# A two-layer convolution kernel: the fill of layer 0 in a written order

## The chip, the cores and the metric

The kernel runs on one core of a Trainium2 chip. The engines are named as the profile names them: PE (TensorE, matrix products; PEld is its weight load), DVE (VectorE), ACT (ScalarE), POOL (GpSimd) and SP (SyncE, which here only issues DMAs; ACT issues some too). The metric is the device time of one execution in microseconds, and of several executions the median.

## What is computed

The input `x` is two images of 512 channels and 64 x 64 pixels, float32. Two layers follow each other, both with a group norm in front and a residual:

```
x = x + L0(_gn(x))       # _gn: 32 groups, mean and variance over channels of a group and all pixels
x = x + L1(_gn(x))

L0:  xproj  = x^T @ in_w + in_b                       # 512 -> 512 per pixel
     x1     = depthwise 3x3 conv of x, + dw_b         # per channel
     x1     = gelu(layernorm over channels(x1) * ln_g + ln_b)
     offset = x1 @ off_w + off_b                      # 16 groups x 9 points x 2
     mask   = softmax over 9 points of (x1 @ mask_w + mask_b)
     out    = bilinear samples of zero-padded xproj at 9 shifted points, weighted by mask
     out    = out @ out_w + out_b

L1:  q, k   = tanh(x Wq^T), tanh(x Wk^T);  attn = softmax(q diag(align_w) k^T) over 4096 pixels
     out    = relu(batchnorm((x + attn @ (x Wv^T)) Wfc^T + bfc))
```

## The kernel before

**Tiling.** Channels lie on 128 partitions in `KB` = 4 blocks. An image is cut into `NCH` = 8 chunks of `CH` = 512 pixels (`ROWS` = 8 image rows), so layer 0 has `NSEQ` = 16 chunks. All of it is float32. `window_path` (the function that the change touches) does layer 0 and then layer 1; a second path for unusual data, `general_path`, is not taken here.

**Stages of layer 0**, each a Python generator whose `yield`s cut it into steps:

- `image_stats(n)`: a `bn_stats` (L723) for each of 32 pieces of an image, `bn_aggr` for each channel block, and the small chain of `group_norm_steps` (L609 to L627: two tiny products with `gmat`, a root on ACT), which leaves scale and bias (L731, L732). Image 0 is loaded whole at the start into `img` (L661, L662: two tiles lie over `bt`, two in the `patch` slots) and its statistics read that. Image 1's pieces come one by one by ACT-issued DMAs (L721) into three places (`early` twice, and `xraw`).
- `project(i)`: chunk i with a row above and below is normalized on ACT into `xn` (L758; there is one `xn` for all chunks), then four products `pq` with `in_w` (L768), each copied by ACT to one of two `xj` tiles (L774) and stored to `xt_d` in DRAM (L776). Chunk 0 reads its pixels from `img`; all other chunks load them again into `raw` tiles (L747).
- `features(i)`: the depthwise convolution of `xn` into `a` (tag `conv`, one buffer): tap 1 on ACT (L793), eight more taps for each channel block on DVE (L798), a sum over blocks on POOL (L804, L806), the mean by a product with `ones` on PE (L811), subtraction (L816, DVE), squares (L819, ACT), sums (L822, L824, POOL), the variance on PE, its root (L828, ACT), reciprocal and scaling (L830, L831, DVE), Gelu (L835, ACT) into `feat` (one buffer).
- `weights(i)`: four products `po` with the offset and mask weights (L852), bias (L857, DVE), exponential (L864, ACT), tent functions and products (L869 to L900, DVE), a copy (L903, ACT) and transposes (L911, PE).
- `fetch(i, s)`: SP loads 8 patches from `xt_d` into a `patch` tile (L924).
- `sample(i)`: spreads the weights (`pb` L940, `bt` L945), gathers by products with the patches (`pa` L959, copies L970), applies `out_w` (`py` L979), adds the input (L984), takes layer 1's statistics (L985) and stores.
- `value_weights()`: layer 1's product of `Wv` and `Wfc`: `wv` and `wf` are loaded (L1106, L1107) into the two `dT` buffers, and four groups of products `pw` (L1111) are copied to `res` tiles (L1115) and stored.
- `output_bias()`: `in_b` through `out_w` (L1123), added to `out_b`.

The zero padding of the projected image is made by the 16 stores of `edge` (L701, L702) into the border of `xt_d`.

**Order.** Within `tc.manual_schedule()` every engine gets its instructions in the order in which the program is traced. There, `period` interleaves four chunks: sampling of chunk i (`m`), weights of i+1 (`w`), features of i+2 (`f`), projection of i+3 (`p`), the rest of the chunk before (`y`, `v`), and six calls of `more`, each a step of image 1's statistics. Outside of it a planner puts the traced instructions of each engine in an order of its own, after its own model of their times. The fill, which brings chunks 0 to 2 to where the first period begins, is planned in this way:

```
run(image_stats(0), project(0), value_weights(), features(0), project(1))
v = Chain(weights, 0)
v(23)
run(features(1), project(2), output_bias())
fetch(0, 0)
fetch(0, 1)
later, y, f = image_stats(1), Chain(sample, NSEQ), Chain(features, 2)
with tc.manual_schedule():
    f()
    for i in range(NSEQ):
        if i == NCH - 3:
            run(later)
```

`Chain(stage, i)(k)` runs the next k steps of a stage. At i = 5 the remaining steps of image 1's statistics run at once, because chunk 8, the first of image 1, is projected in that period.

Of the kernel before, what the change touches and what calls it, by code (L numbers as in the profile page):

```python
# [9 lines left out]
F32 = mybir.dt.float32  # L10
# [7 lines left out]
P = 128  # L18
NB = 2
C = 512  # L20
KB = C // P
H = W = 64
# [8 lines left out]
CH = 512  # L31
NCH = S // CH
ROWS = CH // W
# [537 lines left out]
def window_path(ctx: ExitStack, tc: tile.TileContext, t_in: dict, out: bass.AP, far: bass.AP, sums: bass.AP):  # L571
# [12 lines left out]
    def load(name, shape, src=None, pool=const, **kw):  # L584
        t = pool.tile(shape, F32, name=f"{name}_sb", **kw)
        nc.sync.dma_start(t, t_in[name] if src is None else src)
        return t
# [49 lines left out]
    with ExitStack() as l0:  # L637
# [39 lines left out]
        nc.gpsimd.tensor_copy(om_b, om_b0.rearrange("p (a g k) -> p a k g", a=3, k=NP))  # L677
        out_w = load_w("L0_conv_out_w", C, wp)
        out_b = load("L0_conv_out_b", [P, KB], None, wp)
        ones = wp.tile([P, P], F32, name="ones_c")  # L680
        nc.vector.memset(ones, 1.0 / C)

# [10 lines left out]
            id32[:, :NW].rearrange("p (y x) -> p y x", x=5),  # L693
        )

        edge = io.tile([P, C], F32, tag="res", name="edge", bufs=4)
        nc.sync.dma_start(edge, t_in["L0_conv_in_b"].partition_broadcast(P))
        nc.vector.tensor_scalar(edge, edge, -1.0, None, ALU.mult)
        for n in range(NB):
            for e in (0, 1, WIN - 2, WIN - 1):  # L700
                nc.sync.dma_start(xt_d[n][e], edge[:WIN, :])  # L701
                nc.sync.dma_start(xt_d[n][2 : H + 2, e, :], edge[:H, :])  # L702

        gn = {}

        def image_stats(n):

            mv = sm.tile([P, KB, 2], F32, name="gn_mv")
            room = [early[:, 0], early[:, 1], io.tile([P, CH], F32, name="xraw")] if n else []
            pieces, ahead = deque((kb, h) for kb in range(KB) for h in range(NCH)), deque()  # L710
            for kb in range(KB):
                st = sm.tile([P, NCH, 6], F32, name="gn_st")
                for h in range(NCH):
                    if n == 0:
                        t = img[kb][:, h * CH : (h + 1) * CH]
                    else:

                        while len(ahead) < 3 and pieces:
                            k2, h2 = pieces.popleft()
                            ahead.append(room[len(pieces) % 3])  # L720
                            nc.scalar.dma_start(ahead[-1], x_v[n, :, k2, h2 * CH : (h2 + 1) * CH])  # L721
                        t = ahead.popleft()
                    nc.vector.bn_stats(st[:, h, :], t)  # L723
                    yield
                nc.vector.bn_aggr(mv[:, kb, :], st.rearrange("p a b -> p (a b)"))
            yield
            result = []
            yield from group_norm_steps(mv, KB, sm, ps, result)
            sc, bi = result
            gn[n] = [sm.tile([P, KB], F32, name=f"gn_{k}{n}") for k in ("scale", "bias")]  # L730
            nc.vector.tensor_copy(gn[n][0], sc)  # L731
            nc.vector.tensor_copy(gn[n][1], bi)  # L732

        def project(i):

            n, ch = divmod(i, NCH)
            sc, bi = gn[n]
            lo, hi = max(ch * ROWS - 1, 0), min(ch * ROWS + ROWS + 1, H)
            r0 = lo - (ch * ROWS - 1)
            raws = deque()  # L740

            def read(kb):
                if i == 0:
                    raws.append(img[kb][:, lo * W : hi * W].rearrange("p (r c) -> p r c", c=W))
                else:
                    t = io.tile([P, ROWS + 2, W], F32, name="raw", bufs=3)
                    nc.sync.dma_start(t[:, : hi - lo, :].rearrange("p r c -> p (r c)"), x_v[n, :, kb, lo * W : hi * W])  # L747
                    raws.append(t[:, : hi - lo, :])

            for kb in range(3):  # L750
                read(kb)
            yield
            if ch == 0:
                nc.gpsimd.memset(xn[:, :, 0, :], 0.0)
            if ch == NCH - 1:
                nc.gpsimd.memset(xn[:, :, ROWS + 1, :], 0.0)
            for kb in range(KB):
                nc.scalar.activation(  # L758
                    xn[:, kb, r0 : r0 + hi - lo, :], raws.popleft(),
                    AF.Identity, bias=bi[:, kb : kb + 1], scale=sc[:, kb : kb + 1],  # L760
                )
                if kb + 3 < KB:
                    read(kb + 3)
                yield
            for t in range(ROWS // 2):
                pq = ps.tile([P, C], F32, tag="mm", name="pq")
                for kb in range(KB):
                    nc.tensor.matmul(  # L768
                        pq, xn[:, kb, 1 + 2 * t : 3 + 2 * t, :].rearrange("p r c -> p (r c)"), in_w[:, kb, :],
                        start=(kb == 0), stop=(kb == KB - 1),  # L770
                    )
                yield
                xj = io.tile([P, C], F32, name="xj", bufs=2)
                nc.scalar.copy(xj, pq)  # L774
                for r in range(2):
                    nc.sync.dma_start(xt_d[n][2 + ch * ROWS + 2 * t + r, 2 : W + 2, :], xj[r * W : (r + 1) * W, :])  # L776
                yield
# [2 lines left out]

        def features(i):

            a = cv.tile([P, KB, CH], F32, tag="conv", name="conv")
            def tap_of(kb, tap):
                dy, dx = tap // 3, tap % 3 - 1
                acc = a[:, kb, :].rearrange("p (r c) -> p r c", c=W)
# [4 lines left out]
            for kb in range(KB):  # L791
                dst, src, wt = tap_of(kb, 1)
                nc.scalar.activation(dst, src, AF.Identity, bias=dw_b[:, kb : kb + 1], scale=wt)  # L793
            yield
            for kb in range(KB):
                for tap in (0, 2, 3, 4, 5, 6, 7, 8):
                    dst, src, wt = tap_of(kb, tap)
                    nc.vector.scalar_tensor_tensor(dst, src, wt, dst, ALU.mult, ALU.add)  # L798
                    if tap < 8:
                        yield  # L800

                if kb == 1:
                    tot = sm.tile([P, CH], F32, tag="tot", name="tot")
                    nc.gpsimd.tensor_add(tot, a[:, 0, :], a[:, 1, :])  # L804
                elif kb > 1:
                    nc.gpsimd.tensor_add(tot, tot, a[:, kb, :])  # L806
                yield
# [181 lines left out]
        def run(*generators):  # L989
            for gen in generators:  # L990
                for _ in gen:
                    pass
# [109 lines left out]

        def value_weights():

            wv, wf = [cv.tile([P, KB, C], F32, tag="dT", name=name, bufs=2) for name in ("wv", "wf")]
            nc.sync.dma_start(wv, t_in["L1_conv_Wv"].rearrange("(kb p) m -> p kb m", p=P))  # L1106
            nc.sync.dma_start(wf, t_in["wfcT"].rearrange("(kb p) m -> p kb m", p=P))  # L1107
            for cb in range(KB):
                pw = ps.tile([P, C], F32, tag="mm", name="pw")
                for kb in range(KB):  # L1110
                    nc.tensor.matmul(  # L1111
                        pw, wv[:, kb, cb * P : (cb + 1) * P], wf[:, kb, :], start=(kb == 0), stop=(kb == KB - 1)
                    )
                t = io.tile([P, C], F32, tag="res", name="wc_part", bufs=4)
                nc.scalar.copy(t, pw)  # L1115
                nc.sync.dma_start(wc_d[:, cb, :], t)
                yield
# [9 lines left out]
            nc.vector.tensor_add(out_b, out_b, pb[:, :KB])  # L1127
            yield

        run(image_stats(0), project(0), value_weights(), features(0), project(1))  # L1130
        v = Chain(weights, 0)
        v(23)
        run(features(1), project(2), output_bias())
        fetch(0, 0)
        fetch(0, 1)
        later, y, f = image_stats(1), Chain(sample, NSEQ), Chain(features, 2)
        with tc.manual_schedule():
            f()
            for i in range(NSEQ):
                if i == NCH - 3:  # L1140
                    run(later)
                    for k, name in enumerate(("wkT", "wqT", "wkT")):
                        nc.sync.dma_start(wkq[:, :, k, :], t_in[name].rearrange("(kb p) m -> p kb m", p=P))
                    for h in range(2):
                        nc.sync.dma_start(al[h * DQ : (h + 1) * DQ, :], t_in["L1_conv_align_w"])
                w, m, g = Chain(weights, i + 1), Chain(sample, i), Chain(features, i + 3)
                if i + 2 >= NSEQ:
                    (next_to_last if i + 1 < NSEQ else last_period)(y, v, m, w)
                    y, v = m, w
                    continue  # L1150
                period(y, v, m, w, f, g, Chain(project, i + 3), lambda: next(later, None))
                y, v, f = m, w, g
            y.rest()

# [442 lines left out]
```

## Time and profile before

| | us |
|---|---|
| median of 3 runs | 3677.05 |
| lowest and highest | 3676.55, 3680.48 |
| the profiled execution | 3680.32 |
| its span, first to last instruction | 3678.2 |

| engine | busy us | share of the span |
|---|---|---|
| PE | 3412.8 | 93% |
| DVE | 2351.4 | 64% |
| ACT | 1306.7 | 36% |
| POOL | 292.7 | 8% |

The mean granted TensorE clock is 0.973. A timeline has start and duration in us, engine, line, operation, output and inputs, and in brackets the idle time of the engine before it with what ended it. "SPq" and "ACTq" are DMA issues on SP and ACT. A table of stretches has from left to right the stretch, its length, busy time (and count) of PE, PEld, DVE, ACT and POOL, the granted clock, the busy share of the DMA engines, and GB/s. A list of waits has who waited for whom, the sum in us, how often, and the longest. The float32 products count as two records each on PE.

### The profile page before, as it was taken

To read this page: it belongs to the slowest core of one execution; us is meant where nothing else is said; L and a number is where in the kernel's file an instruction comes from. 1 tells how busy PE (TensorE), PEld (TensorE's weight loads), DVE (VectorE), ACT (ScalarE), POOL (GpSimd) and SP (SyncE) were. 2 spreads that over 40 slices of the span, in tenths; PEclk is the share of its full clock that TensorE was granted. 3 is DMA by queue.
4 is the path that set the end of the run, shared out by engine and by line. 5 is a ranking of instruction groups with operands and counts; after the bars stand their busy time and mean duration, and the time that the engine had idled before them with its cause. 6 is when DMAs were issued, how large, how long until landed. Compare 5 with 4: busy or idle time off the path is not lost.

```text
span 3678.2 us, 38948 instructions
## 1 busy us (share of the span) xinstructions
PE 3412.8 (93%) x15155; PEld 2432.7 (66%) x15155; DVE 2351.4 (64%) x3549; ACT 1306.7 (36%) x1694; POOL 292.7 (8%) x190
## 2 busy tenths in 40 slices
PE   4689998999998999999999999999999999999990
PEld 1355555555555677777777777777777777777770
DVE  5699999999997575554554554477455455545544
ACT  2477786887886421111111111121111111111114
POOL 2112111212111020000000000021000000000000
PEclk9799999999999999999999999999999999999995
DMA  7233442442432445334333433434333343343349
GB/s 241 66 98 112 142 138 83 121 128 85 129 107 71 154 171 180 124 103 163 122 119 134 143 123 113 153 146 187 130 126 116 115 139 112 102 150 122 112 177 379
DMA packets 175044, 499.92 MB, mean 136 GB/s; under 512 B 21600, under 2 KB 55136, under 8 KB 165376
## 3 DMA queue, kind: packets, MB, share of 16 engines
q1 hardware_dynamic: 166464, 462.72, 37.2%
q10 hardware_dynamic: 8352, 34.61, 2.6%
q8 instruction: 121, 1.98, 0.2%
q14 instruction: 75, 0.61, 0.0%
q0 software_dynamic: 32, 0.00, 0.0%
HBM read 405.96 MB, written 91.29 MB: 135 GB/s over the span
## 4 chain that ended last, share of the span: by engine, by line
PE 78%; DVE 13%; DMA 4%; ACT 2%; issue 1%; POOL 1%; SPq 1%; ACTq 0%; DVEq 0%; POOLq 0%
PE acc L1423 42%; DVE conv L798 9%; PE pS L1268 7%; PE p L1466 6%; PE py L979 5%; PE pq L768 5%; PE pa L959 5%; PE pv L1308 3%; PE pk L1362 1%; PE p_mean L811 1%; DVE o L857 1%; DMA v<-wv 1%; DMA in_w<-in_L_conv_in_w 1%; DMA xraw<-in_x 0%; DMA r<-wc 0%
## 5 line engine op out<-in xcount | busy, mean ns | idle before, releaser
L1423 PE MATMUL acc<-e,v 128*128 128x256 f32 x3072 | 768.3, 386 | 0.0
L1272 ACT ACTIVATE e<-pS 128x1024 f32<-128x1024 f32 x256 | 262.1, 1024 | 1386.9 <-PE pS L1268 1318.4
L1423 PE MATMUL acc<-tt,v 128*128 128x256 f32 x3072 | 748.2, 380 | 0.9 <-DMA v<-wv 0.9
L1423 PEld LDWEIGHTS acc<-e,v 128*128 128x128 f32 x3072 | 566.8, 190 | 232.9 <-issue 165.3
L1423 PEld LDWEIGHTS acc<-tt,v 128*128 128x128 f32 x3072 | 582.7, 190 | 91.4 <-issue 10.6
L1275 DVE TENSOR_TENSOR t<-e 128x256 f32<-128x256 f32 x256 | 109.0, 426 | 762.3 <-ACT e L1272 762.3
L798 DVE SCALAR_TENSOR_TENSOR conv<-xn,L_conv_dw_w_sb,conv 128x504 f32<-128x504 f32 (+1 forms) x512 | 400.2, 796 | 42.8 <-ACT conv L793 30.8
L1285 DVE TENSOR_TENSOR tot<-tot,e 128x512 f32<-128x512 f32 x480 | 330.2, 688 | 8.3
L959 PEld LDWEIGHTS pa<-bt,patch 96*128 96x128 f32 x2048 | 252.6, 198 | 62.2 <-issue 34.8
L1268 PE MATMUL pS<-q,kq 64*128 64x512 f32 x1024 | 289.0, 641 | 0.0
L959 PE MATMUL pa<-bt,patch 96*128 96x128 f32 x2048 | 256.3, 282 | 12.2 <-ACT dT L970 5.8
L945 ACT COPY bt<-pb 96x1024 f32<-96x1024 f32 x124 | 234.6, 2007 | 61.2 <-PE pb L940 52.3
L768 PE MATMUL pq<-in_w,xn 128*128 128x512 f32 x512 | 236.4, 606 | 4.0 <-ACT xn L758 4.0
L979 PE MATMUL py<-dT,L_conv_out_w_sb 128*128 128x512 f32 x512 | 236.1, 606 | 0.0
L1466 PE MATMUL p<-t,v 128*128 128x256 f32 x1024 | 231.4, 382 | 1.1 <-DMA v<-wv 1.1
L1466 PEld LDWEIGHTS p<-t,v 128*128 128x128 f32 x1024 | 192.3, 190 | 47.6 <-issue 21.2
L970 ACT COPY dT<-pa 32x256 f32<-32x256 f32 x496 | 179.5, 362 | 69.1 <-PE pa L959 60.3
L852 PE MATMUL po<-om_w_pg,feat 128*128 128x432 f32 x512 | 203.3, 543 | 0.0
L979 PEld LDWEIGHTS py<-dT,L_conv_out_w_sb 128*128 128x128 f32 x512 | 98.2, 196 | 118.9 <-issue 115.0
L768 PEld LDWEIGHTS pq<-in_w,xn 128*128 128x128 f32 x512 | 94.4, 195 | 109.0 <-issue 93.1
L852 PEld LDWEIGHTS po<-om_w_pg,feat 128*128 128x128 f32 x512 | 93.8, 192 | 90.9 <-issue 89.9
L1268 PEld LDWEIGHTS pS<-q,kq 64*128 64x128 f32 x1024 | 77.1, 184 | 84.9 <-issue 84.9
(206 smaller groups left out, 3730.9 us busy)
## 6 DMA issues: line engine op xcount, KB each, us to landing
v<-wv SPq DMA_DIRECT2D x252, 768.0 KB
patch<-xt SPq DMA_DIRECT2D x256, 192.0 KB
v<-wv SPq DMA_DIRECT2D x256, 128.0 KB
wv<-v SPq DMA_DIRECT2D x32, 896.0 KB
xt<-xj SPq DMA_DIRECT2D x128, 128.0 KB
res<-in_x SPq DMA_DIRECT2D x64, 256.0 KB
wx<-res SPq DMA_DIRECT2D x64, 256.0 KB
xq<-wx SPq DMA_DIRECT2D x16, 1024.0 KB
```

The source lines that it names most:

```text
L768: nc.tensor.matmul(pq, xn[:, kb, 1 + 2 * t : 3 + 2 * t, :].rearrange("p r c -> p (r c)"), in_w[:, kb, :], start=(kb == 0), stop=(kb == KB ...
L798: nc.vector.scalar_tensor_tensor(dst, src, wt, dst, ALU.mult, ALU.add)
L852: nc.tensor.matmul(po[:, : 3 * GP], f[:, kb, t * P : (t + 1) * P], om_w[:, kb].rearrange("p a k g -> p (a k g)"), start=(kb == 0), stop=(k ...
L945: copy(bt[:SN].rearrange("s g q d -> s d (g q)")[:, d0 : d0 + 4, :], pb[:SN])
L959: nc.tensor.matmul(pa[:, p], xp[:SN, p, cb * P : (cb + 1) * P], bt[:SN, 4 * cb : 4 * cb + 4, PX * s + p, :], start=True, stop=True,)
L970: copy(dst, src)
L979: nc.tensor.matmul(py, out_w[:, kb, cb * P : (cb + 1) * P], dT[:, kb, :], start=(kb == 0), stop=(kb == KB - 1))
L1268: nc.tensor.matmul(pS[:, h, :], kq[r, 2 * (kp // 4) + h, c0 : c0 + P], qs[qb][r, :], start=True, stop=True)
L1272: nc.scalar.activation(e.rearrange("p a q -> p (a q)"), pS.rearrange("p h q -> p (h q)"), AF.Exp)
L1285: nc.vector.tensor_add(tots[qb], tots[qb], e2[:, h, :])
L1423: nc.tensor.matmul(acc[j][:, cb * HQ : (cb + 1) * HQ], v[:, j, cb * P : (cb + 1) * P], ops[j], start=(kp + cb == 0), stop=(kp + cb == NPAI ...
L1466: nc.tensor.matmul(p7[:, cb * HQ : (cb + 1) * HQ], v7[:, cb * P : (cb + 1) * P], t3, start=(k + cb == 0), stop=(k + cb == NPAIR + 2),)
```

## The change

The fill is written out by hand. Only the loads, small preparations and `image_stats(0)` stay with the planner. The parts:

- `wv` and the four quarters of `wf` are loaded at the start, ahead of `edge`: `wv` into a `dT` buffer, `wf` into the four `res` tiles. `value_weights` makes its four quarters one at a time, where it is called, and copies them to `xj` tiles instead of `res`.
- `edge` lies in a `raw` tile, and its 16 stores are a function `border`, called after chunk 0's projection.
- Chunks 0, 1 and 2 all read their pixels from `img`.
- The convolution of chunk 1 has a buffer of its own (a `dT` slot), and its sum over channels lies in a `raw` tile, so that it can be made while chunk 0's convolution is still normalized.
- `features(0)` and `features(1)` yield after each block of tap 1, so that the blocks of normalization and tap 1 alternate on ACT.
- `image_stats(1)` has one more step, which sends the first three loads; it and eight pieces are taken in the fill.

The diff without its unchanged lines and some renamings:

```diff
+        wv = cv.tile([P, KB, C], F32, tag="dT", name="wv", bufs=2)
+        nc.sync.dma_start(wv, t_in["L1_conv_Wv"].rearrange("(kb p) m -> p kb m", p=P))
+        wf = [io.tile([P, C], F32, tag="res", name="wf", bufs=4) for _ in range(KB)]
+        for kb in range(KB):
+            nc.sync.dma_start(wf[kb], t_in["wfcT"][kb * P : (kb + 1) * P, :])
...
-        edge = io.tile([P, C], F32, tag="res", name="edge", bufs=4)
+        edge = io.tile([P, ROWS + 2, W], F32, name="raw", bufs=3).rearrange("p r c -> p (r c)")[:, :C]
         nc.sync.dma_start(edge, t_in["L0_conv_in_b"].partition_broadcast(P))
         nc.vector.tensor_scalar(edge, edge, -1.0, None, ALU.mult)
-        for n in range(NB):
-            for e in (0, 1, WIN - 2, WIN - 1):
-                nc.sync.dma_start(xt_d[n][e], edge[:WIN, :])
-                nc.sync.dma_start(xt_d[n][2 : H + 2, e, :], edge[:H, :])
+        def border():
+            for n in range(NB):
+                for e in (0, 1, WIN - 2, WIN - 1):
+                    nc.sync.dma_start(xt_d[n][e], edge[:WIN, :])
+                    nc.sync.dma_start(xt_d[n][2 : H + 2, e, :], edge[:H, :])
...
+            def refill():
+                while len(ahead) < 3 and pieces:
+                    k2, h2 = pieces.popleft()
+                    ahead.append(room[len(pieces) % 3])
+                    nc.scalar.dma_start(ahead[-1], x_v[n, :, k2, h2 * CH : (h2 + 1) * CH])
+            if n:
+                refill()
+                yield
...
-                if i == 0:
+                if i < 3:
                     raws.append(img[kb][:, lo * W : hi * W].rearrange("p (r c) -> p r c", c=W))
...
-            a = cv.tile([P, KB, CH], F32, tag="conv", name="conv")
+            a = cv.tile([P, KB, CH], F32, tag="dT", name="conv", bufs=2) if i == 1 else cv.tile([P, KB, CH], F32, tag="conv", name="conv")
...
-            yield
+                if i < 2 or kb == KB - 1:
+                    yield
...
+                    if i == 1:
+                        tot = io.tile([P, ROWS + 2, W], F32, name="raw", bufs=3).rearrange("p r c -> p (r c)")[:, :CH]
+                    else:
+                        tot = sm.tile([P, CH], F32, tag="tot", name="tot")
...
-                t = io.tile([P, C], F32, tag="res", name="wc_part", bufs=4)
+                t = io.tile([P, C], F32, tag="xj", name="wc_part", bufs=2)
...
-        run(image_stats(0), project(0), value_weights(), features(0), project(1))
-        v = Chain(weights, 0)
-        v(23)
-        run(features(1), project(2), output_bias())
-        fetch(0, 0)
-        fetch(0, 1)
+        run(image_stats(0))
         later, y, f = image_stats(1), Chain(sample, NSEQ), Chain(features, 2)
+        def more():
+            next(later, None)
         with tc.manual_schedule():
+            p0, p1, p2 = [Chain(project, i) for i in range(3)]
+            f0, f1, v, products = Chain(features, 0), Chain(features, 1), Chain(weights, 0), value_weights()
+            p0()
+            for kb in range(KB):
+                p0()
+                f0()
+            for t in range(4):
+                p0(2)
+                f0(8)
+            border()
+            more()
...
```

The remaining calls are, in this order (one call to a word, the number of steps in brackets): p1(3), f1, product, p1, f1(2), product, p1, f1, f1(6), f0(2), p1(4), f1(12), f0, p1(2), f0, p1, f0(2), p1, f1(14), product, p2(5), f; four times v, more, more, v; fetch of both patch tiles of chunk 0; f1, v, f1, v, p2(2), v(2), p2(2), v, f1, v(3), p2(2), f1, p2, f1(2), p2, v(6), product, output bias, v. The step counts: `project` has 1 to 5 for reading and normalizing and then two for each of four products; `features(0)` and `features(1)` have 4 for tap 1, 32 for the taps on DVE, then mean, squares, root, scaling, and two for Gelu. The periods follow as before, with `more` in them.

More of the change, by code (lines that the diff above doesn't have):

```diff
@@ L716, in image_stats @@
                     else:
[L718 to L721, printed above, removed]
+                        refill()
                         t = ahead.popleft()
@@ L802, in features @@
                 if kb == 1:
-                    tot = sm.tile([P, CH], F32, tag="tot", name="tot")
+                    if i == 1:
+                        tot = io.tile([P, ROWS + 2, W], F32, name="raw", bufs=3).rearrange("p r c -> p (r c)")[:, :CH]
+                    else:
+                        tot = sm.tile([P, CH], F32, tag="tot", name="tot")
                     nc.gpsimd.tensor_add(tot, a[:, 0, :], a[:, 1, :])
@@ L1103, in value_weights @@
         def value_weights():
-            wv, wf = [cv.tile([P, KB, C], F32, tag="dT", name=name, bufs=2) for name in ("wv", "wf")]
-            nc.sync.dma_start(wv, t_in["L1_conv_Wv"].rearrange("(kb p) m -> p kb m", p=P))
-            nc.sync.dma_start(wf, t_in["wfcT"].rearrange("(kb p) m -> p kb m", p=P))
             for cb in range(KB):
@@ L1111, in value_weights @@
                     nc.tensor.matmul(
-                        pw, wv[:, kb, cb * P : (cb + 1) * P], wf[:, kb, :], start=(kb == 0), stop=(kb == KB - 1)
+                        pw, wv[:, kb, cb * P : (cb + 1) * P], wf[kb], start=(kb == 0), stop=(kb == KB - 1)
                     )
-                t = io.tile([P, C], F32, tag="res", name="wc_part", bufs=4)
+                t = io.tile([P, C], F32, tag="xj", name="wc_part", bufs=2)
                 nc.scalar.copy(t, pw)
@@ L1128, in output_bias @@
             yield
-        run(image_stats(0), project(0), value_weights(), features(0), project(1))
-        v = Chain(weights, 0)
-        v(23)
-        run(features(1), project(2), output_bias())
-        fetch(0, 0)
-        fetch(0, 1)
+        run(image_stats(0))
         later, y, f = image_stats(1), Chain(sample, NSEQ), Chain(features, 2)
+        def more():
+            next(later, None)
         with tc.manual_schedule():
-            f()
+            p0, p1, p2 = [Chain(project, i) for i in range(3)]
[9 more added lines that the diff above has]
+            more()
+            p1(3)
+            f1()
+            next(products)
+            p1()
+            f1(2)
+            next(products)
+            p1()
+            f1()
+            f1(6)
+            f0(2)
+            p1(4)
+            f1(12)
+            f0()
+            p1(2)
+            f0()
+            p1()
+            f0(2)
+            p1()
+            f1(14)
+            next(products)
+            p2(5)
+            f()
+            for t in range(4):
+                v()
+                more()
+                more()
+                v()
+            fetch(0, 0)
+            fetch(0, 1)
+            f1()
+            v()
+            f1()
+            v()
+            p2(2)
+            v(2)
+            p2(2)
+            v()
+            f1()
+            v(3)
+            p2(2)
+            f1()
+            p2()
+            f1(2)
+            p2()
+            v(6)
+            next(products)
+            run(output_bias())
+            v()
             for i in range(NSEQ):
@@ L1150, in window_path @@
                     continue
-                period(y, v, m, w, f, g, Chain(project, i + 3), lambda: next(later, None))
+                period(y, v, m, w, f, g, Chain(project, i + 3), more)
                 y, v, f = m, w, g
```

## The prediction

> **What bounds the kernel now.** I read the slices of the span first, then busy time by stretches, then VectorE's (DVE's) waits and its instructions in order of time in the fill, and last the queues that its releasers stand in.
>
> ```profile
> PE   4689998999998999999999999999999999999990
> DVE  5699999999997575554554554477455455545544
> ...
> 0.00:92.00 92.00, 40.23 (x76) 17.48 (x77) 49.72 (x89) 18.46 (x27) 25.38 (x20) 0.91 0.70 241
> 92.00:184.00 92.00, 56.13 (x169) 28.59 (x167) 64.36 (x73) 41.86 (x47) 13.32 (x9) 0.74 0.24 66
> 251.00:322.00 71.00, 65.99 (x308) 38.98 (x308) 66.78 (x79) 54.01 (x73) 13.04 (x9) 0.98 0.41 130
> 1240.00:1900.00 660.00, 652.34 (x2798) 495.43 (x2798) 365.87 (x672) 123.09 (x156) 29.48 (x12) 1.00 0.41 144
> ```
>
> A slice is 92 us. From slice 3 DVE stands at 9 (a period of 71 us has 66.8 us of it: 94%), from about 1240 us TensorE (PE) at 99%. Only the first two slices are loose: DVE has 49.7 and 64.4 us of 92, and no other engine is full. So the fill is a matter of order and waits; whatever it sheds reaches the end, because a full engine follows all the way. Where DVE stands still:
>
> ```profile
> DVE conv L816 <- PE p_mean L811: 18.1, 1, 18.1
> DVE rstd L830 <- ACT rstd L828: 13.2, 2, 8.1
> DVE conv L798 <- ACT conv L793: 11.4, 2, 7.5
> DVE L_conv_out_b_sb L1127 <- PE p_bias L1123: 8.7, 1, 8.7
> DVE gn_st L723 <- DMA early<-in_x: 5.9, 1, 5.9
> ...
> 36.11 0.43 DVE L698 TENSOR_SCALAR edge<-edge 128x512 f32<-128x512 f32 x1 [1.38 <-DMA edge<-in_L_conv_in_b]
> 40.60 21.14 DVE L798 SCALAR_TENSOR_TENSOR conv<-xn,L_conv_dw_w_sb,conv 128x504 f32<-128x504 f32 x32 [3.91 <-ACT conv L793]
> 79.84 2.29 DVE L816 TENSOR_TENSOR conv<-conv,p_mean 128x2048 f32<-128x2048 f32 x1 [18.09 <-PE p_mean L811]
> 179.06 0.69 DVE L723 BATCH_NORM_STATS2 gn_st<-early 128x6 f32<-128x512 f32 x1 [5.87 <-DMA early<-in_x]
> 246.21 3.09 DVE L798 SCALAR_TENSOR_TENSOR conv<-xn,L_conv_dw_w_sb,conv 128x504 f32<-128x504 f32 x4 [3.02 <-ACT conv L793]
> ```
>
> The 18.09 us before L816 come from elsewhere:
>
> ```profile
> 51.33 11.54 POOL L804 TENSOR_TENSOR tot<-conv 128x512 f32<-128x512 f32 x1 [16.62 <-DVE conv L798]
> 56.24 0.54 SPq L1107 DMA_DIRECT2D wf<-in_wfcT  x1
> 62.35 16.59 PE L1111 MATMUL pw<-wf,wv 128*128 128x512 f32 x32 [7.70 <-issue]
> ```
>
> SP sends 16 border stores from 36.6 to 52.4, then pixel stores, and only at 56.2 wf. All 32 records of the weight product wait for it on PE, and p_mean, whose sum is ready at 65.6, starts at 78.8. One more loose place lies past the fill:
>
> ```profile
> 534.14 1.28 ACT L622 ACT_TABLE_LOAD   x1
> 535.76 0.18 DVE L625 RECIPROCAL gn_sc<-gn_var 128x4 f32<-128x4 f32 x1 [4.62 <-ACT gn_var L622]
> ```
>
> There the rest of image 1's statistics runs in one piece: the first taps of successive convolutions lie 71.2 us apart (317.02, 388.22), this one 76.8 behind its forerunner (459.45 by the chain of waits, to 536.25).
>
> **What the Trainium skill says.** "SBUF — State Buffer", section "Who interferes with whom": a DVE instruction with two SBUF inputs and a GpSimd (POOL) instruction that reads SBUF exclude each other for a whole instruction. The trace agrees: the add at 51.33 took 11.54 us beside DVE's unbroken taps against 1.26 us alone; later, taps held up by an add take 1.66 instead of 0.74 us. "VectorE: DVE Perf Modes", section "The DRAIN you can't avoid": a semaphore after each operation costs a chain nothing. Here it differs: at 40.60 taps of two channel blocks alternate (the 504 and 512 shapes come in pairs) and each takes 0.66 us; at 179.67 and 246.21 taps of one block follow each other, at 0.78. "DMA: Bandwidth & Descriptors", section "Queues, rings and completion order": SP's and ACT's queues take turns on the same DMA engines. The trace: at 324.6 an ACT piece of 256 KB took 6.16 us beside SP's patches, at 176.1 one took 2.98.
>
> **The change, part by part**, as DVE's queue, which is what the fill waits for.
>
> *Loads.* wv and four wf, 2.1 MB, now stand before edge on SP. From 27 to 36 us the queue moved about 0.33 MB per us, so edge lands 6.3 us later, at 42.4, and L698 ends at 42.9. All later DVE work queues behind it. ACT's normalization needs 1.6 us from 36.7 to the first tap at 38.3, so 4.6 us are lost if L698 stands last in the unwritten part, and 6.8 if it stays before the copies L731 and L732 as now. I take 42.9. The product's operands are then there before it is called.
>
> *First convolution.* Written block by block: 32 taps at 0.78, 24.8, plus two POOL adds at 0.9: 42.9 to 69.5. That is 3.7 slower than the alternating order, but without POOL's starvation. PE's 13.8 us of pq and ACT's four copies lie beside it; the border's 16 stores come behind the pixel stores, about 57 to 73.
>
> *Second convolution between.* It has its own buffer (the dT slot of om_b) and its own sum, so while the first waits for means DVE does its taps. Six taps 4.7 + 0.9: 75.1 (first means: sum 70.8, matmul 72.9, hidden). L816 2.2: 77.3. Twelve taps 9.4 and four POOL adds 3.6: 90.3; beside them the squares, POOL, the variance and ACT's root, due about 87. L830 and L831 5.6: 95.9. Fourteen taps 10.9 + 0.9: 107.7. The waits of 18.1, 8.1 and 7.5 are gone. Raw loads of chunks 1 and 2 (20 DMAs) go; their data is in the image. Three quarters of the product, 3.4 us each (16.59 over 4 is 4.1, with a first wait), lie on PE under these taps.
>
> *Weights of chunk 0 and eight statistics.* Eight bn_stats at 0.6 and four o additions at 0.52: 6.9. Gelu ends about 102, the four po of 3.2 us about 115: just covered. The pieces are the unknown. Three are loaded ahead; the fourth's DMA is behind ACT's last tap copies, about 111, exactly when SP starts 16 patch loads (3.1 MB). A piece then takes 3 to 6 us and two must follow one another (fourth, then seventh): 3 to 16 us of stall. I take 8: 122.6. Queued behind are both statistics and o, and behind them Exp on ACT.
> Then L816 2.2; tx 3.4, sums and scaling 3.3, my 3.0, first five aw operations 4.8 (rows at 209 to 223 us with POOL among them): 139.3. L830 and L831 5.6; twelve aw operations at 0.79, 9.5: 154.4. Chunk 2's pq (13.8), the last product quarter and the output bias lie on PE under it; at (2.9) and the four p_tr follow on ACT and PE, as in a steady period (251.8, 5.6 us behind the taps).
>
> *The first period* begins on DVE at 154.4 instead of 179.07, without a wait for `early`: **24.7 us less**. Its own DVE work is unchanged.
>
> *Later.* Image 1's statistics need 39 steps; one refill and eight are done in the fill, and five periods call 30. So the run before period 5 finds nothing, and the fifth period has six bn_stats less (3.7) and 1.0 of small operations more: 71.2 - 3.7 + 1.0 = 68.5 against 76.8, **8.3 less**. The root of this norm follows the convolution's root on ACT, so it needs no table load of its own ("ScalarE: Activation LUTs", section "What ACT_TABLE_LOAD costs", gives 1283 ns; the trace 1.28).
>
> Sum: -33.0. The profiled execution took 3680.32 (span 3678.2 and 2.1 around it), so 3647.3; the runs' median is 3.3 lower, 3677.05, and gives **3644**.
>
> **Rivals.**
> A, *nothing is late*: edge hides (4.6) and pieces arrive in time (8): -45.6, 3631. For it: in later periods pieces cost DVE 1.2 us in all. Against: there they are asked for many taps ahead.
> B, *transfers are later than I think*. The product's parts and the pixel copies share two xj slots, and the first copies of chunk 1 (about 79) wait for stores behind the border on SP, free about 76. Were the border to take 32 us instead of 16, ACT's root would be held to 95, 4 us past DVE's need; with 16 us at the pieces instead of 8: +12, 3656. For it: ACT waited 9.0 us for just such a slot at 57.4. Against: the covering 3 us, and the sum of squares, which leaves slack.
> C, *slower: the granted clock*. From 1240 us PE is full for 2440 us at a granted 1.00; it falls to 0.80 in the fill when PE starts and stops. If earlier dense work took 1.4% from the grant in that stage, 33 us are gone; from there on the kernel is slower, at 2% (+49) 3660 becomes 3693. Against: the dense periods up to 1240 us ran at 0.96 to 0.98, and the grant still returned to 1.00.
> D, *same*: the stretches after the fill absorb it. Against: DVE at 94% of the periods.
>
> **How the numbers follow.** Mine 0.60, A 0.15, B 0.15, C 0.07, D 0.03. A measurement of this kernel tells no change from about 0.2%, 7 us. The range takes in A and B with the bounds of the pieces (3 to 16) and of edge: 3630 to 3660. Faster 0.90, same 0.03, slower 0.07.
>
> **What would show it.** DVE's first tap near 43 with L698's wait of about 6 us before it; taps 0.78 apart; no wait over 3 us until 107; waits for `early` or `xraw` of some 8 us between 107 and 123; the first tap of chunk 3's convolution near 221 instead of 246; no L622 wait at the sixth period. I am wrong if DVE waits for PE or ACT for more than 5 us at L816 or L830, if border stores hold xj, or if the grant past 1240 us falls below 0.99.

## The result, and the profile after

| | before | after |
|---|---|---|
| median of 4 runs, us | 3676.8 | 3639.97 |
| lowest and highest | 3675.86, 3680.48 | 3638.82, 3641.34 |
| profiled execution | 3680.32 | 3641.34 |
| its span | 3678.2 | 3639.5 |

The ratio is 0.9898, with a 95% interval from 0.9881 to 0.9915: the medians lie 36.8 us apart, the two profiled executions 39.0. The forecast was 33.0 less, 3644.

The page of the kernel after, its 40 slices (91 us each):

```profile
PE   5789999999998999999999999999999999999990
DVE  8899999999995674554555455476455545545544
```

DVE's first two slices stand at 8 where they were 5 and 6; PE's gain a tenth each. The table of stretches says how much:

```profile
0.00:92.00 92.00, 46.54 (x98) 19.90 (x98) 77.61 (x112) 26.11 (x36) 17.33 (x20) 0.96 0.62 211
92.00:184.00 92.00, 67.18 (x252) 36.47 (x252) 77.08 (x94) 49.48 (x52) 17.91 (x12) 0.83 0.33 97
1210.00:1870.00 660.00, 654.49 (x2817) 499.51 (x2815) 366.94 (x680) 122.19 (x154) 29.50 (x12) 1.00 0.40 141
```

In the first 92 us DVE works 77.6 us (49.7 before), in the next 77.1 (64.4). From 1210 us the stage of layer 1 is as before, PE at 99% with a granted clock of 1.00. Of DVE's waits in the first 180 us, those that bear on the fill:

```profile
DVE gn_st L738 <- DMA early<-in_x: 12.0, 4, 5.6
...
DVE conv L814 <- ACT conv L808: 1.8, 1, 1.8
...
DVE gn_st L738 <- DMA xraw<-in_x: 0.9, 1, 0.9
```

Of the four largest waits of before (18.1, 13.2, 11.4 and 8.7 us) 1.8 are left. The fifth, for a piece of image 1, has grown from 5.9 to 12.9 in all. DVE in order of time:

```profile
36.91 4.65 DVE L814 SCALAR_TENSOR_TENSOR conv<-xn,L_conv_dw_w_sb,conv 128x504 f32<-128x504 f32 x6 [1.83 <-ACT conv L808]
41.48 0.42 DVE L704 TENSOR_SCALAR raw<-raw 128x512 f32<-128x512 f32 x1
41.81 27.15 DVE L814 SCALAR_TENSOR_TENSOR conv<-xn,L_conv_dw_w_sb,conv 128x512 f32<-128x512 f32 x32
68.88 2.28 DVE L835 TENSOR_TENSOR conv<-conv,p_mean 128x2048 f32<-128x2048 f32 x1
71.08 12.78 DVE L814 SCALAR_TENSOR_TENSOR conv<-xn,L_conv_dw_w_sb,conv 128x512 f32<-128x512 f32 x12
83.78 3.34 DVE L849 RECIPROCAL rstd<-rstd 128x512 f32<-128x512 f32 x1
...
89.36 11.65 DVE L814 SCALAR_TENSOR_TENSOR conv<-xn,L_conv_dw_w_sb,conv 128x504 f32<-128x504 f32 x14
...
108.96 0.69 DVE L738 BATCH_NORM_STATS2 gn_st<-early 128x6 f32<-128x512 f32 x1 [5.64 <-DMA early<-in_x]
...
118.75 0.69 DVE L738 BATCH_NORM_STATS2 gn_st<-early 128x6 f32<-128x512 f32 x1 [4.54 <-DMA early<-in_x]
...
151.48 0.69 DVE L738 BATCH_NORM_STATS2 gn_st<-xraw 128x6 f32<-128x512 f32 x1
```

From 36.9 to 102 us there is no wait at all. L835 (the L816 of before) and L849 (L830) carry no bracket: both come behind the second convolution's taps, with mean and root already there. The first period begins at 151.1 instead of 179.06. The pieces are asked for by ACT while SP sends all the patches of chunk 0:

```profile
97.87 19.05 SPq L943 DMA_DIRECT2D patch<-xt  x16
...
102.07 0.34 ACTq L725 DMA_DIRECT2D early<-in_x  x1
```

The first tap of successive convolutions, read from the same view of both kernels (us):

| chunk of the convolution | before | after | less |
|---|---|---|---|
| 2 | 179.67 | 152.10 | 27.6 |
| 3 | 246.21 | 217.75 | 28.5 |
| 6 | 459.48 | 430.44 | 29.0 |
| 7 | 536.25 | 498.57 | 37.7 |
| 8 | 605.52 | 566.31 | 39.2 |
| 15 | 1079.51 | 1040.31 | 39.2 |

So 27.6 us come from the fill and 10.2 from the two intervals between chunks 6 and 8, where image 1's norm no longer runs in one piece; nothing is won or lost after that. The 1.4 us between chunks 2 and 6 were not traced to the change: periods of equal work differ by more than that within one trace (after chunk 3, 71.5 us at a granted clock of 0.98, then 69.7 at 1.00).

### The profile page after: what moved, and what is told of

Same layout as the page of the kernel before. It is cut to its first block, busy times and chain, and to the rows that moved or that the text cites. A ratio compares the mean times of both kernels' runs of the same rounds, so it can differ in the third digit from the quotient of the medians.

```text
span 3639.5 us, 38933 instructions
## 1 busy us (share of the span) xinstructions
PE 3406.3 (94%) x15155; PEld 2428.3 (67%) x15155; DVE 2356.1 (65%) x3549; ACT 1305.9 (36%) x1693; POOL 284.7 (8%) x190
## 4 chain that ended last, share of the span: by engine, by line
PE 77%; DVE 15%; DMA 4%; ACT 2%; issue 1%; POOL 1%; SPq 0%; ACTq 0%; DVEq 0%; POOLq 0%
PE acc L1497 42%; DVE conv L814 10%; PE pS L1342 7%; PE p L1540 6%; PE py L998 6%; PE pq L783 5%; PE pa L978 5%; PE pv L1382 3%; PE pk L1436 1%; DMA early<-in_x 1%; PE p_mean L830 1%; DMA v<-wv 1%; DVE o L876 1%; DMA in_w<-in_L_conv_in_w 1%; DMA out<-ct 0%
## 5 line engine op out<-in xcount | busy, mean ns | idle before, releaser
L814 DVE SCALAR_TENSOR_TENSOR conv<-xn,L_conv_dw_w_sb,conv 128x504 f32<-128x504 f32 (+1 forms) x512 | 409.3, 807 | 35.4 <-ACT conv L808 21.5
L978 PE MATMUL pa<-bt,patch 96*128 96x128 f32 x2048 | 255.0, 281 | 12.9 <-ACT dT L989 5.8
L1342 PEld LDWEIGHTS pS<-q,kq 64*128 64x128 f32 x1024 | 77.1, 184 | 84.9 <-issue 84.9
```

The source lines that it names most:

```text
L978: nc.tensor.matmul(pa[:, p], xp[:SN, p, cb * P : (cb + 1) * P], bt[:SN, 4 * cb : 4 * cb + 4, PX * s + p, :], start=True, stop=True,)
L1342: nc.tensor.matmul(pS[:, h, :], kq[r, 2 * (kp // 4) + h, c0 : c0 + P], qs[qb][r, :], start=True, stop=True)
```

## The experiments

All are the kernel after with one edit, except where the kernel before is named; medians, with lowest and highest run. The kernel before took 3677.5 and 3678.1 beside them. The kernel after was not run again, so its 3639.97 stands for it. For edge first, no pieces and alternating taps in chunk 0 the intervals of the ratio to the kernel before overlap with that of the kernel after (0.9881 to 0.9915): there the traces, not the times, carry the reading.

**edge ahead of the first tap.** Line L704 moves into the written part, ahead of the first call:

```diff
-        nc.vector.tensor_scalar(edge, edge, -1.0, None, ALU.mult)
...
         with tc.manual_schedule():
             p0, p1, p2 = [Chain(project, i) for i in range(3)]
+            nc.vector.tensor_scalar(edge, edge, -1.0, None, ALU.mult)
```

> The changed kernel took 3640 us, with the scaling of edge standing behind the sixth tap, where it found edge just landed (about 41.5 us). Here it stands ahead of the first tap. Theory A (the fill is DVE's chain, and only that place hid the later landing): the first tap moves from 36.9 to about 41.8, everything behind it shifts by the same 4.9 less the two waits that follow from transfers, and the kernel takes 3644 to 3645. Rival (the fill waits further on for transfers and PE, which do not move): 3640, with the loss made up by shorter waits for image 1's pieces near 105 to 120 us.

3644.09 (3641.76 to 3646.35). DVE in order of time:

```profile
40.55 0.43 DVE L1154 TENSOR_SCALAR raw<-raw 128x512 f32<-128x512 f32 x1 [4.91 <-DMA raw<-in_L_conv_in_b]
40.90 4.64 DVE L813 SCALAR_TENSOR_TENSOR conv<-xn,L_conv_dw_w_sb,conv 128x504 f32<-128x504 f32 x6
```

The bracket is the wait for edge that the forecast had put there. The first tap is 4.0 later, chunk 3's first tap 3.6 later (221.37), the kernel 4.1. Waits further on take up only 0.4 of the loss.

**Pieces early.** Six statistics between the taps, two among the bias additions:

```diff
-            f1(12)
+            f1(2)
+            more()
+            f1(5)
+            more()
+            f1(5)
+            more()
...
-            f1(14)
+            for taps in (5, 5, 4):
+                f1(taps)
+                more()
...
-                more()
-                more()
+                if t % 2 == 0:
+                    more()
```

> Six of the eight statistics of image 1 are taken between the second convolution's taps, two stay among the four bias additions; nothing else moves. Theory A (the 12.8 us that DVE waits for pieces between 102 and 121 us are made by asking for them on ACT behind the tap copies, just when SP sends 16 patch loads): the waits for early and xraw fall under 2 us, the first period starts on DVE near 139 instead of 152, and the kernel takes 3626 to 3628. Rival (the four products with the offset weights, or chunk 2's projection on PE, would end as late): part of the wait comes back at the bias additions or at the root of the variance, and the kernel stays at 3634 or more.

3628.57 (3624.62 to 3630.87), just above A's 3626 to 3628. Two of DVE's waits in the first 180 us:

```profile
DVE o L876 <- PE po L871: 2.7, 2, 2.2
DVE conv L814 <- ACT conv L808: 1.8, 1, 1.8
```

No line of `early` or `xraw` is left, and chunk 2's first tap comes at 138.87, 13.2 earlier than in the kernel after. The rival's waits for PE are small in the fill: 0.8 us. Only 9.7 of the 13.2 are left at chunk 3 (208.02): its period is 69.2 long instead of 65.7. Of these 3.5 us, 2.2 are a wait for PE, whose first `po` takes longer than the usual 3.17 (PE had stood idle for 9.6 us shortly before; why the product is slower there was not tried), and 1.3 a longer wait for ACT's taps at chunk 3. PE in order of time:

```profile
147.27 4.19 PE L871 MATMUL po<-om_w_pg,feat 128*128 128x432 f32 x8
```

**The second convolution's taps after the first's normalization.** The same buffers, another order:

```diff
             f1()
-            f1(6)
             f0(2)
             p1(4)
-            f1(12)
             f0()
...
-            f1(14)
+            f1(32)
```

> The 32 taps of the second convolution are called after the first one's normalization and Gelu instead of between its steps; the buffers, loads and the rest of the order stay. Theory A (its own buffer is worth the waits for means that these taps cover): DVE waits about 4 us for the first mean and about 8 for the root, the kernel takes 12 to 14 us more, 3652 to 3654. Rival (the fill's gain comes from the product's place and its early operands alone): within 3 us of 3640.

3651.32 (3649.0 to 3654.24): 11.4 more, just under A's lower end. DVE in order of time shows the two waits that A named, 3.58 and 8.19 us.

```profile
67.53 2.29 DVE L835 TENSOR_TENSOR conv<-conv,p_mean 128x2048 f32<-128x2048 f32 x1 [3.58 <-PE p_mean L830]
78.00 3.35 DVE L849 RECIPROCAL rstd<-rstd 128x512 f32<-128x512 f32 x1 [8.19 <-ACT rstd L847]
```

Part of their 11.8 us comes back: the second convolution takes 26.3 us in one piece, 29.7 in the three pieces of the kernel after, where more of POOL's adds fall among the taps. Chunk 2's first tap is 8.5 later (160.57).

**Chunk 1 from DRAM.**

```diff
-                if i < 3:
+                if i in (0, 2):
```

> Chunk 1 reads its pixels from DRAM again, by loads that SP sends behind the border's stores; chunk 2 stays with the image. Theory A (SP's border keeps the loads back until about 73 us, and ACT's squares stand behind the normalization they feed): ACT's first normalization of chunk 1 moves from 54 to about 76, DVE waits 12 to 16 us more, and the kernel takes 3653 to 3657. Rival (the loads are hidden, as all others of their kind are in the periods): 3640 to 3642.

3656.74 (3654.13 to 3659.46), as A has it. First ACT in order of time, then DVE's waits:

```profile
77.32 1.73 ACT L773 ACTIVATE xn<-raw,gn_bias,gn_scale 128x640 f32<-128x640 f32 x2 [24.05 <-DMA raw<-in_x]
```

```profile
DVE conv L814 <- ACT conv L808: 17.8, 2, 16.0
```

ACT stands 24 us for a load whose data lies in SBUF already: the load is behind the border on SP, as SP's order shows (`xt<-raw` is the last border store):

```profile
71.47 0.45 SPq L710 DMA_DIRECT2D xt<-raw  x1
71.96 6.63 SPq L762 DMA_DIRECT2D raw<-in_x  x4
```

This is the largest single loss found.

**The kernel before, with the product's operands early.**

```diff
+        wv, wf = [cv.tile([P, KB, C], F32, tag="dT", name=name, bufs=2) for name in ("wv", "wf")]
+        nc.sync.dma_start(wv, t_in["L1_conv_Wv"].rearrange("(kb p) m -> p kb m", p=P))
+        nc.sync.dma_start(wf, t_in["wfcT"].rearrange("(kb p) m -> p kb m", p=P))
         edge = io.tile([P, C], F32, tag="res", name="edge", bufs=4)
...
-            wv, wf = [cv.tile([P, KB, C], F32, tag="dT", name=name, bufs=2) for name in ("wv", "wf")]
-            nc.sync.dma_start(wv, t_in["L1_conv_Wv"].rearrange("(kb p) m -> p kb m", p=P))
-            nc.sync.dma_start(wf, t_in["wfcT"].rearrange("(kb p) m -> p kb m", p=P))
```

> The kernel before (3677 us), with one edit: wv and wf are both loaded ahead of edge and its border stores, so that the product's operands are there; the planner orders the rest as it does. Theory A (of the fill's waits, the 18.1 us ahead of the first subtraction are the product's, standing on PE ahead of the mean until wf comes): that wait falls to 2 to 6 us and the kernel takes 3663 to 3667. Rival (PE's order or the planner's new plan puts another wait there): 3672 or more.

3671.83 (3668.55 to 3675.46), ratio 0.9984 (0.9976 to 0.9993): 6 us less, about half of what A expected, and next to the rival's 3672. DVE's waits:

```profile
DVE rstd L833 <- ACT rstd L831: 19.1, 2, 14.0
...
DVE conv L819 <- PE p_mean L814: 6.5, 1, 6.5
```

The wait at the mean falls from 18.1 to 6.5, and the next one, at the root, grows from 8.1 to 14.0: both theories have a share. What is left at the mean is POOL's adds, ready at 64.4, and 1.6 us of the product still ahead of it on PE:

```profile
61.80 2.61 POOL L809 TENSOR_TENSOR tot<-tot,conv 128x512 f32<-128x512 f32 x2
66.02 1.02 PE L814 MATMUL p_mean<-tot,ones_c 128*128 128x512 f32 x2
```

ACT in order of time shows why the wait at the root grows:

```profile
73.68 1.74 ACT L761 ACTIVATE xn<-raw,gn_bias,gn_scale 128x640 f32<-128x640 f32 x2 [6.49 <-DMA raw<-in_x]
75.32 2.17 ACT L822 ACTIVATE feat<-conv 128x512 f32<-128x512 f32 x4
```

The squares could start at 69.4, when the subtraction ends. They start 5.9 us later, since they stand behind two normalizations of chunk 1, whose pixels SP asks for only at 68.5, behind the border's stores and those of chunk 0's pixels and of the product. So in the kernel before the late operands made 11.6 of the 18.1 us at the mean, and once they are early the late pixels add 5.9 at the root. Both stood in SP's queue behind the same 16 stores. That is read from its order; a kernel in which only the border moves was not run.

**No pieces in the fill.**

```diff
             for t in range(4):
-                v()
-                more()
-                more()
-                v()
+                v(2)
```

> The changed kernel without the eight statistics in the fill (three loads are still sent early); two statistics and the norm's chain of image 1 run at once ahead of the sixth period, as in the kernel before. Theory A (the pieces cost the fill 4.9 us of DVE and 12.8 us of waits, and give 10.2 us back in the fifth and sixth period): 17.7 less, 10.2 more, so 3632 to 3634. Rival (the fill has other waits behind these, and what is saved later is more than the statistics): 3640 or more.

3635.72 (3634.46 to 3639.16): faster than the kernel after by 4.3, where A had 6 to 8 and the rival nothing. By the first taps, chunk 2 is 15.5 earlier (136.62), chunk 3 14.6 (203.17) and chunk 8 only 3.8 (562.47): 10.8 us are given back, nearly all between chunks 6 and 8, for 10.2 expected. The gain in the fill was the term that was too large (15.5 for 17.7); in place of the pieces, DVE waits 1.9 us for `po` and 0.3 for a mean.

**Alternating taps in chunk 0**, the same edit in the next kernel for more chunks:

```diff
+            taps = (0, 2, 3, 4, 5, 6, 7, 8)
+            order = [(kb, tap) for kb in range(KB) for tap in taps]
+            if i in PAIRED:
+                order = [(kb + k, tap) for kb in (0, 2) for tap in taps for k in range(2)]
+            for kb, tap in order:
```

> The changed kernel with the taps of chunk 0's convolution on two channel blocks in turn (blocks 0 and 1, then 2 and 3) instead of block by block. Theory A (taps that follow on their own result take 0.78 us, alternating ones 0.66): the second convolution's first tap moves from 63.4 to about 59.5 and the kernel takes 3636 to 3637; POOL's first add is held for some 10 us and costs nothing, since the first mean is due behind six more taps. Rival (the order of the taps makes no difference in a written order, or the held sums give it back): 3640, or up to 3 us more.

3641.12 (3636.81 to 3644.15): the runs spread over more than the effect, so the time decides nothing. The trace does decide about the pace: the second convolution's first tap is at 59.13 (63.4 in the kernel after), chunk 2's at 149.65 (152.1). POOL in order of time:

```profile
48.80 12.22 POOL L828 TENSOR_TENSOR tot<-conv 128x512 f32<-128x512 f32 x1 [14.70 <-DVE conv L818]
61.10 3.24 POOL L830 TENSOR_TENSOR tot<-tot,conv 128x512 f32<-128x512 f32 x2
```

The first add is held for 12.2 us, much as in the kernel before. It costs no wait at the mean, but all three adds then block taps of the second convolution instead of one. So the 1.8 us of the other two are only moved, and of 4.3 us 2.4 are left at chunk 2.

**Pieces early and alternating taps** in chunks 0 and 2 to 7 (`PAIRED`), both edits above together:

> The kernel with pieces early (3628.6) and alternating taps in chunk 0 and chunks 2 to 7. Theory A (the periods of image 0 hang on DVE, busy 66.5 of 71 us): 3.8 us less for chunk 0 and about 3 for each of the next five, 3610 to 3616. Rival (PE, busy 64 to 66 us of each period, takes over as soon as DVE is faster, or POOL's sums come too late): 3 to 6 us in all, 3622 to 3626.

3616.07 (3611.01 to 3618.82), ratio to the kernel before 0.9827 (0.981 to 0.9843): the fastest, 24 us below the kernel after and at the upper end of A. Stretches between first taps of chunks 3, 4 and 5:

```profile
202.34:272.29 69.95, 66.19 (x309) 39.01 (x308) 64.70 (x79) 53.89 (x73) 13.44 (x9) 0.98 0.41 131
272.29:340.87 68.58, 64.55 (x309) 38.33 (x308) 64.60 (x79) 53.87 (x73) 13.43 (x9) 1.00 0.42 133
```

A period is 1.1 to 2.5 us shorter than with pieces early alone, not 3: DVE's busy time (third number after the length) falls by 2 us, and PE, the first number, is now as busy as DVE. Theory and rival both have a share: chunk 2's first tap gains 3.2 us, and six periods, not five, bring 9.7 where A had about 15.

## Why the prediction was right

By its own steps, against the trace of the profiled execution:

| step | forecast, us | measured |
|---|---|---|
| first tap (edge) | 42.9 | 36.9 |
| 32 taps and two POOL adds | 26.6 | 26.5 |
| six taps, one add, to the subtraction | 5.6 | 5.4 |
| subtraction and twelve taps | 15.2 | 14.9 |
| reciprocal, scaling, fourteen taps | 17.4 | 17.2 |
| eight statistics and four additions | 6.9 and 8 of wait | 20.1 in all, 12.8 of it wait |
| weights of chunk 0, up to the root | 16.7 | 15.0 |
| reciprocal to the first period | 15.1 | 15.0 |
| first period begins | 154.4 | 151.1 |
| later, image 1's norm | -8.3 up to chunk 7 | -8.6 from chunk 6 to 7, -10.8 from chunk 3 to 8 |

- *What bounds the fill.* Right. What moved DVE's chain by more than the spread of the runs moved the end: +11.4 without the second convolution's taps to cover the waits, +16.8 with chunk 1 loaded, -11.4 with the pieces early. For the 4.0 us of edge first the median (+4.1) agrees; the 2.4 of alternating taps in chunk 0 are lost in the spread.
- *Edge.* The mechanism is right, the step is wrong. I let all DVE work of the fill queue behind L698 (now L704). The planner put it behind the sixth tap of the written part: planned and written instructions share one queue and mix. It waited for nothing there. The term is 0 instead of 4.6 over the ideal start, and the start itself was 1.4 earlier than I had it. Even with edge first the scaling began at 40.55, so edge also landed earlier than my 42.4.
- *Pieces.* Right in place, too small. From being asked for to being used, the five pieces that DVE waited for took 6.4 to 7.3 us (the one of 102.07 until 108.96), where I had taken 3 to 6. With two of them in series 12.8 us were lost, not 8. The pieces-early kernel shows that the wait is a matter of place alone.
- *Luck.* The two errors have opposite signs, 6.0 and 4.8, and nearly cancel. The total came as close as it did in part by luck.
- *Alternating against chained taps.* Right: 0.78 in the fill after, and with the taps in turn 32 of them ended 4.3 us earlier, 1.8 of it adds that only moved. What in the chain costs the 0.12 us, the semaphore or something else, no run here shows.
- *The later part.* The interval to chunk 7 went from 76.77 to 68.13 (forecast 68.5). The next one also fell, from 69.27 to 67.73, which I had not counted. Without the pieces in the fill both are back together: 146.6 against 146.0 before and 135.9 after.
- *Rivals.* A's hidden edge came true, its hidden pieces did not. B's mechanism is there, and with it one sign of being wrong, that stores on SP hold `xj`: ACT's first copy of chunk 1 waits 4.65 us for a stored quarter of the product and its root ends at 79.9. But DVE needs it at 83.8, so it costs nothing; the pieces, at 12.8 us, lie between my 8 and B's 16. C: the grant past 1210 us stayed at 1.00. D: 39.2 us at chunk 8 are 39.2 at chunk 15.
- *Two slips in the working.* C's last sum starts from 3644, not 3660 (3644 and 49 are 3693). And the piece of 324.6 ran beside loads of `raw`, which SP issues from 322.8, and not beside patches alone. The first does not touch the forecast; the second is the higher of the two times that I had for a piece.
- *What carries the gain.* I put the 18.1 us at the mean down to the product; its late operands made 11.6 of them, POOL's held adds and the mean most of the rest. Moving the operands alone brought 6 us, since the late pixels of chunk 1 then showed. That the image serves chunk 1 is worth 16.8 (chunk 2 was not tried alone), the cover by the second convolution 11.4. These single losses are not parts of one sum: each was measured with all other parts in place, and a wait removed alone lets the next one show. Undoing the border's place was not tried.

## What to carry to other kernels

When an engine stands still, ask what queue its releaser stood in and what else stands behind the same spot: one block of stores stood ahead of the product's operands and of chunk 1's pixels, and through them held up the mean and the squares; freeing one of them only showed the next. A loop of load, use and refill belongs between long work, not where another queue starts a burst. In a fill, give the engine that will be the bound a second, independent piece of work (here for the price of one buffer), and look at its brackets in order of time until none is left.

## What was not expected of the hardware

A transfer on one DMA queue can take more than twice as long when the other queue is busy: a 256 KB piece on ACT's queue needed 6.4 to 7.3 us while SP's patch loads ran, and 2.98 in the kernel before at 176.1, as SP sent its last pixel store. What the patches lost was not measured. In these traces alternating taps without gaps keep POOL's add out until they end (12.2 us with alternating taps in chunk 0, 11.5 in the kernel before). A chain of dependent taps at 0.78 lets each add through in 1.64 to 1.72 us, against 1.26 alone, and the tap beside it then takes 1.63 to 1.66 us instead of 0.74. The slower chain starves nobody.
